# A two-layer graph network on one core: ten of 25 adjacency banks moved beside the products, degrees from one-hots, edge keys by 40 matmuls, x read in fewer pieces

## The chip, the cores and the metric

The kernel runs on one core of a Trainium2 chip. The metric is the device time of one execution in microseconds, the median of several runs. One execution of each kernel is also recorded by the hardware profiler; its page and its trace give the times of single instructions.

## The reference

1250 nodes with 512 features, 20000 edges (`src`, `dst`, sorted by `dst`), two layers. What matters here is the first:

```python
h = jnp.maximum(_layernorm(x, axis=-1), 0.0)          # 1250 x 512
xn = _batchnorm(h, norm1_g, norm1_b)
agg = jax.ops.segment_sum(xn[src], dst, num_segments=N)
deg = jax.ops.segment_sum(jnp.ones((E,)), dst, num_segments=N)
conv_out = relu(agg / jnp.maximum(deg, 1.0)[:, None] @ W_conv + b_conv)
# linear attention (8 heads, random features) over the first 256 nodes: q, k, v from h
x = x + _batchnorm(conv_out + h_attn + h, norm2_g, norm2_b)
# second layer: h = relu(layernorm(x)); z = (1 + eps) h + segment_sum(h[src], dst);
# two dense layers 512 -> 1024 -> 512 with batch norms; x + result
```

The inputs are float32, the indices int32.

## The kernel before

The kernel turns the edge list into a dense matrix `adj` (sources on partitions, 10 blocks of 128 rows; targets on 1250 columns) and does both segment sums as matmuls with it. It is written with a framework that orders each engine's instructions by itself, by their place in the program and a cost model; `order(...)` (`keep_in_program_order`) pins the order where it is used. Buffers come from pools; a tile of a pool with n buffers waits until the tile n before it is no longer used.

**Prologue** (`tile_gnn`, from L1391). The two edge lists are read into `kd` (targets) and `ks` (sources), 125 partitions with overlapping stretches of 400 edges, on the queues of SP and ScalarE. A comparison (`sample`, `less`, L1468 to L1475) and ten matmuls (`cnt`, L1478) find where each of 125 groups of ten targets begins. `pick` (L1495) is a one-hot of these places, and 3 x 20 matmuls `keys` (L1518) gather for each group a slot of 256 edges: the target, the source modulo 128 and the source's block times 1280. `pi` and `ji` (L1490, L1496) split the sources with integer operations on VectorE. VectorE reads the result from PSUM into `kcol` (column key, L1547) and `prow` (row key, L1549). Between these, ScalarE takes the layer norm of the first 256 nodes (`total`, L1506 to L1546), and dummy matmuls (`keep_up`) keep TensorE busy. POOL writes the number lists `iop`, `iok`, `start`, `first` and `lead`.

**Build** (in `sorted_graph`). A batch is a bank of 50 targets, 25 in all. `onehots` (L202) compares the keys with the number lists on VectorE, giving `op` (128x1280, row) and `ok` (128x1000, column); `count` (L213) multiplies them in ten matmuls of 100 columns into a PSUM tile `acc`, and ScalarE copies it into `adj` (L216). The generator `beside()` yields other work in pieces: transposes of the first nodes, the keys of the attention (`features`, L241 to L256) with the layer norm of further nodes (`node`, L95 to L104, transposed at L222), then eight pairs of scores (L263, copied at L329, maximum at L330) with the values (L333), then the queries with the exponentials of the keys (L372). The loop at L393 runs one batch, then a piece, except after every fourth batch; so all 25 batches are written in the program before the last piece ends.

**Products** (L485 to L500). Ten rounds: `query(i)` (scores, L263; exponentials, L457), `product(i)` (block i of xn W_conv, L413, split into `hi` on ScalarE, L109, and `lo` on VectorE, L110), in round 1 the key-value products (L441), then `turn` (L464) and `attend` (L474). `product` has two PSUM buffers of its own (`hw`), in the place that `acc` has left. `add_degrees` (L423) sums the blocks of `adj` on VectorE, and `degrees` (L428 to L430) sums over partitions with a matmul of ones in three pieces, clips and inverts: `rdeg`.

**After that**, the attention's output (L506 to L518), `adj` times `hi` and `lo` (L567), the second layer. `load_x` reads x in blocks of 128 rows, once for `x1` (rows from 256, L166) and once for `xs` (all rows, L528), on SP's queue.

Of the kernel before, what the change touches and what calls it, by code (L numbers as in the profile page):

```python
# [49 lines left out]
LAST = (E - SLOT) // STEP  # L50
JK = 1280
# [17 lines left out]
def sorted_graph(ctx: ExitStack, tc: tile.TileContext, ed, x, n1g, n1b, n2g, n2b, wconv, bconv,  # L69
# [82 lines left out]

    build = ExitStack()
    edge = build.enter_context(tc.tile_pool(name="edge", bufs=1, side="right"))
    ohp = build.enter_context(tc.tile_pool(name="onehot", bufs=2, side="right"))
    accp = build.enter_context(tc.tile_pool(name="acc", bufs=2, space=PSUM))

    def load_x(t, js):
        for j in js:
            nc.sync.dma_start(t[:ROWS[j], j, :], x[j * S:j * S + ROWS[j], :])  # L160
# [5 lines left out]
    load_x(x1, range(NT, NJ))  # L166
# [27 lines left out]
    def onehots(bt, parts=(BG,)):  # L194
        op = ohp.tile([128, BG, S, 2], F16, name="op")
        ok = ohp.tile([128, BG, NJ * TG, 2], F16, name="ok")
        q = 0
        for n in parts:
            qs = slice(q, q + n)
            for t, keys, iota in ((op, prow, ed.iop), (ok, kcol, ed.iok)):  # L200
                shape = [128, n, iota.shape[1], 2]
                i = nc.vector.tensor_tensor(t[:, qs], iota.unsqueeze(1).to_broadcast(shape),  # L202
                                            keys[:, bt, qs].unsqueeze(2).to_broadcast(shape), ALU.is_equal)
                if len(parts) > 1:
                    order(i)
            q += n
        return op, ok

    def count(bt, op, ok):
        acc = accp.tile([S, NJ, TB], F32, name="acc")  # L210
        for q in range(BG):
            for i in range(2):
                nc.tensor.matmul(acc[:, :, q * TG:(q + 1) * TG], op[:, q, :, i],  # L213
                                 ok[:, q, :, i].rearrange("p (j t) -> p j t", t=TG),
                                 start=(q == 0 and i == 0), stop=(q == BG - 1 and i == 1), skip_group_check=True)
        nc.scalar.copy(adj[:, :, bt * TB:(bt + 1) * TB], acc)  # L216
# [172 lines left out]
    rest = beside()  # L389
    nbt = N // TB  # L390
    ahead = onehots(0, (2, 3))
    next(rest)
    for bt in range(nbt):  # L393
        oh, ahead = ahead, onehots(bt + 1, (BG,) if bt else (2, 3)) if bt + 1 < nbt else None
        count(bt, *oh)
        if bt % 4 != 3:
            next(rest, None)
    for _ in rest:
        pass
# [3 lines left out]
    hwp = att.enter_context(tc.tile_pool(name="hw", bufs=2, space=PSUM, reuse_waits="tile"))  # L403
# [3 lines left out]
    def product(j):  # L407

        n = ROWS[j]
        xn = normed(j, nc.scalar) if j not in xns else xns[j]  # L410
        ps = hwp.tile([S, D], F32, name="hw") if j else mm.tile([S, D], F32, name="mm")
        for f in range(KD):
            nc.tensor.matmul(ps[:n], xn[:, f, :n], wct[:, f, :], start=(f == 0), stop=(f == KD - 1))  # L413
        halves(hi[:n, j, :], lo[:n, j, :], ps[:n])


    onesr = ap1.tile([128, 128], F32R, name="onesr")
    nc.gpsimd.memset(onesr.bitcast(F32), 1.0)
    dsum = lop.tile([S, N], F32R, name="dsum")
    rdeg = lop.tile([128, N], F32, name="rdeg")  # L420

    def add_degrees(j):
        nc.vector.tensor_tensor(dsum, (adj[:, 0, :] if j == 1 else dsum).bitcast(F32), adj[:, j, :].bitcast(F32),  # L423
                                ALU.add)

    def degrees(n0, n):
        ps = mm.tile([128, n], F32, name="mm")
        nc.tensor.matmul(ps, onesr, dsum[:, n0:n0 + n], start=True, stop=True)  # L428
        nc.vector.tensor_scalar(rdeg[:, n0:n0 + n], ps, 1.0, None, op0=ALU.max)
        nc.vector.reciprocal(rdeg[:, n0:n0 + n], rdeg[:, n0:n0 + n])  # L430
# [54 lines left out]
    for i in range(len(pairs) + 2):  # L485
        if i < len(pairs):
            query(i)
        product(i)
        if i == 1:
            for q4 in range(2):  # L490
                keyvalue(0, q4)
                keyvalue(1, q4)
        for j in range(2 * i + 1, min(2 * i + 3, NJ)):
            add_degrees(j)
        if 5 <= i < 5 + len(ESPLIT):
            degrees(*ESPLIT[i - 5])
        if 1 <= i <= len(pairs):
            turn(i - 1)
        if i >= 2:
            attend(i - 2)  # L500
# [27 lines left out]
    load_x(xs, range(NJ))  # L528
# [862 lines left out]
def tile_gnn(ctx: ExitStack, tc: tile.TileContext, x, src, dst, *rest):  # L1391
# [5 lines left out]

    ed.iop = pre.tile([128, S, 2], F16, name="iop")
    ed.iok = pre.tile([128, NJ * TG, 2], I16, name="iok")
    ed.prow = pre.tile([128, NGR, 2], F16, name="prow")  # L1400
    ed.kcol = pre.tile([128, NGR, 2], I16, name="kcol")
    ed.x0 = pre.tile([S, NT, D], F32, name="x0")
# [4 lines left out]
    with tc.tile_pool(name="raw", bufs=1) as raw, tc.tile_pool(name="rawp", bufs=1, space=PSUM) as rawp:  # L1407

        kd, ks = (raw.tile([KS, SPAN], I32, name=name) for name in ("kd", "ks"))
        few = E - (KP - 1) * STEP * RB  # L1410

        def edges(queue, t, v, p0, p1, c0, c1):
            at = bass.AP(tensor=v.tensor, offset=v.offset + p0 * STEP * RB + c0, ap=[[STEP * RB, p1 - p0], [1, c1 - c0]])
            order(queue.dma_start(t[p0:p1, c0:c1], at))

        edges(nc.sync, kd, dst, 0, 96, 0, SPAN)
        edges(nc.scalar, kd, dst, 96, KP, 0, few)
        order(nc.vector.memset(kd[96:KP, few:], 0))
        order(nc.vector.memset(ks[96:KP, few:], 0))
        edges(nc.scalar, kd, dst, KP, KS, 0, STEP * RB)  # L1420
        edges(nc.scalar, kd, dst, 96, KP - 1, few, SPAN)
        edges(nc.sync, ks, src, 0, 96, 0, SPAN)
        edges(nc.sync, ks, src, 96, KP, 0, few)
        edges(nc.sync, ks, src, 96, KP - 1, few, SPAN)
# [9 lines left out]
        ones = raw.tile([KS, 128], F16, name="ones")  # L1434
        one = raw.tile([KP, 1], F32, name="one")
        zero = raw.tile([S, 1], F32, name="zero")
        first = raw.tile([KS, NGR + 1], F16, name="first")
        iota(first, [[TG, NGR + 1]])
        for t, v in ((ones, 1.0), (one, 1.0), (zero, 0.0)):
            order(nc.gpsimd.memset(t, v))  # L1440
        start = raw.tile([KP, RB, 2], F16, name="start")
        iota(start, [[1, RB], [0, 2]], step=RB)
        iota(ed.iok, [[JK, NJ], [1, TG], [0, 2]])
        iota(ed.iop, [[1, S], [0, 2]])
        lead = raw.tile([128, NGR], F32, name="lead")
        iota(lead, [[TG, NGR]])
        order(nc.gpsimd.memset(ed.ident, 0.0))
        make_identity(nc, ed.ident, nomemset=True)

        order(nc.vector.memset(ed.epsc, EPS))  # L1450
        order(nc.vector.memset(ed.zeros, 0.0))
# [25 lines left out]
        for b in range(RB):  # L1477
            order(nc.tensor.matmul(cnt, ones, less[:, b, :], start=(b == 0), stop=(b == RB - 1)))  # L1478


        kd16, pk, jk = (raw.tile([KP, SPAN], F16, name=name) for name in ("kd16", "pk", "jk"))
        order(nc.scalar.copy(kd16, kd[:KP]))
        out = raw.tile([KP, few - 1], F16, name="out")
        wrong = raw.tile([KP, 1], F32, name="wrong")
        order(nc.vector.tensor_tensor(out, kd16[:, :few - 1], kd16[:, 1:few], ALU.is_gt))

        pi, ji = (raw.tile([KP, SPAN], I32, name=name) for name in ("pi", "ji"))
        order(nc.vector.tensor_scalar(pi, ks[:KP], S - 1, None, op0=ALU.bitwise_and))  # L1490
        order(nc.scalar.copy(pk, pi))
# [3 lines left out]
        compared(pick, start, begin, ALU.is_equal)  # L1495
        order(nc.vector.tensor_scalar(ji, ks[:KP], 7, None, op0=ALU.logical_shift_right))  # L1496
        order(nc.vector.tensor_reduce(wrong, out, AX.X, ALU.max))
        wps = rawp.tile([1, 1], F32, name="wps")
        keep_up(4)
# [9 lines left out]
        order(nc.scalar.activation(jk, ji, AF.Copy, scale=float(JK)))  # L1509


        keys = rawp.tile([128, 2, 2, NGR], F32, name="keys")
        parts = ((kd16, 0), (pk, 1), (jk, 0))
        for i, (t, kind) in enumerate(parts):
            for h in range(2):
                for b in range(RB):
                    c = STEP * b + 128 * h
                    order(nc.tensor.matmul(keys[:, kind, h, :], t[:, c:c + 128], pick[:, b, :NGR],  # L1518
                                           start=(i == h == b == 0), stop=(t is jk and h == 1 and b == RB - 1),
                                           skip_group_check=True))  # L1520
            if i == 0:
                order(nc.tensor.matmul(wps, wrong, one, start=True, stop=True))
# [11 lines left out]
        total(AF.Square, acc[:, 0:1], 1.0, 1)  # L1534
# [4 lines left out]
        for j in range(NT):  # L1539
# [4 lines left out]
            else:  # L1544
                order(nc.vector.tensor_tensor(nb[:, 0:1], acc[:, 0:1], r, ALU.mult))
            order(nc.scalar.activation(ed.x0[:, j, :], ed.x0[:, j, :], AF.Relu, bias=nb[:, j:j + 1], scale=r))  # L1546
        order(nc.vector.tensor_tensor(ed.kcol, keys[:, 0].rearrange("p h g -> p g h"),  # L1547
                                      lead.unsqueeze(2).to_broadcast([128, NGR, 2]), ALU.subtract))
        order(nc.vector.tensor_copy(ed.prow, keys[:, 1].rearrange("p h g -> p g h")))  # L1549
# [36 lines left out]
```

## Time and profile before

| what | value |
|---|---|
| median of 3 runs | 377.28 us (377.01 to 377.63) |
| profiled execution | 377.67 us, its span 375.9 us |
| TensorE busy | 358.1 us |
| VectorE busy | 245.3 us |
| ScalarE busy | 157.9 us |
| granted TensorE clock, mean | 0.986 |
| prologue, up to the first one-hot | 0 to 11.9 us |
| build, up to the first block of xn W | 11.9 to 67.3 us |
| products | 67.3 to 126.2 us |
| attention's output | 126.2 to 135.3 us |
| sums with `adj`, second layer | 135.3 us to the end |

Each line of a timeline has its start, its length, the engine, the source line, the operation and the tiles. In a table by stage, each engine has its busy time and, in brackets, its number of instructions. In the chain of work that ended last, each line has a start, a length and what ran; "issue" is time in which an engine waited for nothing that the profile shows. PEld is the loading of weights on TensorE, beside its matmuls (PE).

### The profile page before, as it was taken

The page shows a single profiled execution, that of the slowest core. Times are in us where ns is not written, and L with a number is a line of the kernel's source. Part 1 is how long each engine was busy: PE and PEld are TensorE (multiplying, and loading weights), DVE is VectorE, ACT ScalarE, POOL GpSimd, SP SyncE. Part 2 cuts the span into 40 slices and gives each one's busy share as a digit, 9 for nine tenths or more (in the row PEclk, how much of TensorE's full clock was granted, in tenths as well). Part 3 has the DMA queues.
Part 4 walks back from the last instruction along what each step waited for, and adds up shares of the span by engine and source line. Part 5 has one row for each costly group of instructions (what it writes and reads, how often), then busy time and mean ns, then how long its engine had stood idle before and what let it go on. Part 6 is the DMA issues. An engine that isn't in the chain of part 4 may idle for free.

```text
span 375.9 us, 4974 instructions
## 1 busy us (share of the span) xinstructions
PE 358.1 (95%) x1851; PEld 263.5 (70%) x1851; DVE 245.3 (65%) x579; ACT 157.9 (42%) x308; POOL 37.7 (10%) x56
## 2 busy tenths in 40 slices
PE   7799999999999999999999999999999999999971
PEld 4676556485565789998768888777777777777751
DVE  5899999869689227587887232192780888212883
ACT  5599758835664350111157312232652642111230
POOL 4200000000000005000000009610062000000000
PEclk9999999999999999999999999999999999999995
DMA  6853020000000480000000000240000000000045
GB/s 201 265 202 116 2 112 2 1 2 0 1 2 0 165 305 27 3 0 0 2 0 0 2 0 1 57 168 0 2 0 1 1 2 0 1 2 0 13 123 144
DMA packets 13485, 18.06 MB, mean 48 GB/s; under 512 B 1553, under 2 KB 6858, under 8 KB 13454
## 3 DMA queue, kind: packets, MB, share of 16 engines
q1 hardware_dynamic: 10814, 16.38, 12.8%
q10 hardware_dynamic: 2640, 1.29, 1.4%
q8 instruction: 16, 0.26, 0.3%
q14 instruction: 15, 0.12, 0.1%
HBM read 15.11 MB, written 2.56 MB: 47 GB/s over the span
## 4 chain that ended last, share of the span: by engine, by line
PE 82%; DVE 11%; ACT 4%; issue 1%; DMA 1%; DVEq 0%
PE mm L756 29%; PE mm L699 12%; PE mm L567 12%; PE hw L413 9%; PE mm L241 3%; PE mm L513 2%; PE mm L441 2%; PE mm L474 2%; PE sc L263 2%; DVE op L202 1%; PE acc L213 1%; DVE ok L202 1%; DVE xs L886 1%; PE mm L693 1%; PE mm L413 1%
## 5 line engine op out<-in xcount | busy, mean ns | idle before, releaser
L771 ACT ACTIVATE kept<-mm,vT 128x313 f32<-128x313 f32 x36 | 18.5, 521 | 49.6 <-PE mm L756 48.5
L413 PE MATMUL hw<-wconv,xn 128*128 128x512 f32 (+1 forms) x72 | 33.3, 603 | 0.0
L699 PE MATMUL mm<-hi,adj 128*128 128x512 f32 (+2 forms) x100 | 32.1, 398 | 0.5 <-DVE hi L647 0.4
L699 PE MATMUL mm<-lo,adj 128*128 128x512 f32 (+2 forms) x100 | 31.6, 394 | 0.0
L128 ACT ACTIVATE r<-mv,epsc 128x1 f32<-128x1 f32 x16 | 4.7, 292 | 52.7 <-DVE mv L127 52.7
L567 PE MATMUL mm<-adj,hi 128*128 128x416 f32 (+3 forms) x120 | 25.1, 355 | 0.9 <-DVE hT L517 0.9
L756 PE MATMUL mm<-hid,w 128*128 128x313 f32 x96 | 25.8, 427 | 0.0
L567 PE MATMUL mm<-adj,lo 128*128 128x416 f32 (+3 forms) x120 | 25.0, 354 | 0.0
L776 DVE TENSOR_TENSOR hid<-mm,kept 128x313 f32<-128x313 f32 x24 | 10.9, 477 | 20.4 <-ACT kept L771 16.9
L413 PEld LDWEIGHTS hw<-wconv,xn 128*128 128x128 f32 (+1 forms) x72 | 12.7, 187 | 15.4 <-issue 14.7
L567 PEld LDWEIGHTS mm<-adj,hi 128*128 128x128 f32 x120 | 21.8, 189 | 2.4 <-DVE hT L517 1.3
L756 PEld LDWEIGHTS mm<-hid,w 128*128 128x128 f32 x96 | 18.1, 190 | 6.9
L567 PEld LDWEIGHTS mm<-adj,lo 128*128 128x128 f32 x120 | 21.7, 189 | 1.0
L699 PEld LDWEIGHTS mm<-hi,adj 128*128 128x128 f32 (+2 forms) x100 | 18.4, 186 | 5.7 <-DVE hi L647 1.4
L690 DVE SCALAR_TENSOR_TENSOR z<-h,e,mm 128x512 f32<-128x512 f32 (+1 forms) x10 | 7.0, 744 | 23.5 <-PE mm L699 15.7
L699 PEld LDWEIGHTS mm<-lo,adj 128*128 128x128 f32 (+2 forms) x100 | 18.5, 186 | 4.6 <-DVE lo L640 0.2
L202 DVE TENSOR_TENSOR op<-iop,prow 128x1280 f16<-128x1280 f16 (+2 forms) x27 | 20.5, 759 | 0.6 <-PE acc L213 0.4
L213 PEld LDWEIGHTS <-op 128*128 128x128 f16 x250 | 13.5, 97 | 9.6 <-issue 4.5
L776 DVE TENSOR_TENSOR o<-mm,kept 128x313 f32<-128x313 f32 x12 | 5.7, 481 | 21.5 <-ACT kept L771 20.8
L694 ACT COPY zT<-mm 128x512 f32<-128x512 f32 (+1 forms) x10 | 5.3, 582 | 29.2 <-PE mm L693 29.2
L756 PE MATMUL mm<-tz,w 128*128 128x313 f32 x64 | 17.5, 426 | 0.0
L756 PE MATMUL mm<-hid,sw 128*128 128x313 f32 x64 | 17.5, 426 | 0.0
(252 smaller groups left out, 735.4 us busy)
## 6 DMA issues: line engine op xcount, KB each, us to landing
w<-in_L_gnn_W_dram SPq DMA_DIRECT2D x2, 2048.0 KB
x<-in_x_dram SPq DMA_DIRECT2D x9, 256.0 KB
xs<-in_x_dram SPq DMA_DIRECT2D x9, 256.0 KB
wk<-in_L_gnn_Wk_dram SPq DMA_DIRECT2D x1, 1024.0 KB
v<-in_L_gnn_Wv_dram SPq DMA_DIRECT2D x1, 1024.0 KB
wconv<-in_L_gnn_W_conv_dram SPq DMA_DIRECT2D x1, 1024.0 KB
wk<-in_L_gnn_Wq_dram SPq DMA_DIRECT2D x1, 1024.0 KB
o<-in_L_gnn_Wo_dram SPq DMA_DIRECT2D x1, 1024.0 KB
```

The lines of the kernel that those rows point to most:

```text
L202: i = nc.vector.tensor_tensor(t[:, qs], iota.unsqueeze(1).to_broadcast(shape), keys[:, bt, qs].unsqueeze(2).to_broadcast(shape), ALU.is_equal)
L213: nc.tensor.matmul(acc[:, :, q * TG:(q + 1) * TG], op[:, q, :, i], ok[:, q, :, i].rearrange("p (j t) -> p j t", t=TG), start=(q == 0 and i ...
L241: nc.tensor.matmul(ps, wt[:, k, b * 128:(b + 1) * 128], hT[:, k, :TOK], start=(k == 0), stop=(k == KD - 1))
L263: nc.tensor.matmul(ps[:, a, :M], tT[a * 64:a * 64 + 64, b, t * 128:(t + 1) * 128], projT[a * 64:a * 64 + 64, :], start=True, stop=True)
L413: nc.tensor.matmul(ps[:n], xn[:, f, :n], wct[:, f, :], start=(f == 0), stop=(f == KD - 1))
L441: nc.tensor.matmul(ps[:, i, :], kf[:, t, hd, mb * 128:(mb + 1) * 128], va[:, t, hd, :], start=(t == 0), stop=(t == NT - 1))
L474: nc.tensor.matmul(pa[:, i, :], qfTs[n][:, i, mb, :], kv[:, mb, hd, :], start=(mb == 0), stop=(mb == 1))
L567: nc.tensor.matmul(ps, part[:k, j, fs], adj[:k, j, c], start=(part is hi and j == 0), stop=(part is lo and j == NJ - 1))
L699: nc.tensor.matmul(ps[:n], adj[:k, j, t * S:t * S + n], part[:k, j, :], start=(part is hi and j == 0), stop=(part is lo and j == NJ - 1))
L756: order(nc.tensor.matmul(banks[i], left[:, k, m * 128:(m + 1) * 128], right[:, k, i * NH:(i + 1) * NH], start=(p in (1, 2, 5) and k == 0), ...
L771: nc.scalar.activation(t[:, c, :], self.A[c], AF.Identity, bias=self.part(i, 0, c)[1], scale=1.0)
L776: order(nc.vector.tensor_tensor(self.part(i, j, c)[0], self.B[c], t[:, c, :], ALU.add))
```

## The change

Ten of the 25 batches move from the build to the products, one in each round; `op`, `ok` and `acc` outlive the build, and `acc` and the product's `hw` share one tag with two PSUM buffers:

```diff
+    ohp = att.enter_context(tc.tile_pool(name="onehot", bufs=2))
+    accp = att.enter_context(tc.tile_pool(name="acc", bufs=2, space=PSUM))
     build = ExitStack()
...
+    ready = [onehots(0, (2, 3))]
+    def batch(bt):
+        if bt + 1 < nbt:
+            ready.append(onehots(bt + 1, (BG,) if bt else (2, 3)))
+        count(bt, *ready.pop(0))
     next(rest)
-    for bt in range(nbt):
-        oh, ahead = ahead, onehots(bt + 1, (BG,) if bt else (2, 3)) if bt + 1 < nbt else None
-        count(bt, *oh)
-        if bt % 4 != 3:
-            next(rest, None)
-    for _ in rest:
-        pass
+    batches = iter(range(nbt))
+    for piece in itertools.count():
+        if not 6 <= piece < 14 or piece % 2:
+            batch(next(batches))
+        if next(rest, rest) is rest:
+            break
     build.close()
...
-    hwp = att.enter_context(tc.tile_pool(name="hw", bufs=2, space=PSUM, reuse_waits="tile"))
...
-        ps = hwp.tile([S, D], F32, name="hw") if j else mm.tile([S, D], F32, name="mm")
+        ps = accp.tile([S, D], F32, name="hw", tag="acc")
```

The degrees no longer come from `adj` but from one-hots of the targets within their group of ten, six pieces of up to 21 groups in rounds 2 to 7, with `rdeg` in the memory of `wk`:

```diff
-    def add_degrees(j):
-        nc.vector.tensor_tensor(dsum, (adj[:, 0, :] if j == 1 else dsum).bitcast(F32), adj[:, j, :].bitcast(F32), ALU.add)
-    def degrees(n0, n):
-        ps = mm.tile([128, n], F32, name="mm")
-        nc.tensor.matmul(ps, onesr, dsum[:, n0:n0 + n], start=True, stop=True)
-        nc.vector.tensor_scalar(rdeg[:, n0:n0 + n], ps, 1.0, None, op0=ALU.max)
-        nc.vector.reciprocal(rdeg[:, n0:n0 + n], rdeg[:, n0:n0 + n])
+    rdeg = ed.wk.rearrange("p k n -> p (k n)")[:, :N]
+    def degrees(g0, n):
+        shape = [128, n, TG, 2]
+        oh = tmp.tile(shape, F16, name="oh", tag="row")
+        nc.vector.tensor_tensor(oh, ed.iok[:, :TG, :].unsqueeze(1).to_broadcast(shape),
+                                ed.dist[:, g0:g0 + n].unsqueeze(2).to_broadcast(shape), ALU.is_equal)
+        ps = mm.tile([128, n * TG], F32, name="mm")
+        for i in range(2):
+            nc.tensor.matmul(ps, ed.ones, oh[:, :, :, i].rearrange("p g t -> p (g t)"), start=(i == 0), stop=(i == 1))
+        c = slice(g0 * TG, (g0 + n) * TG)
+        nc.vector.tensor_scalar(rdeg[:, c], ps, 1.0, None, op0=ALU.max)
+        nc.vector.reciprocal(rdeg[:, c], rdeg[:, c])
...
-        for j in range(2 * i + 1, min(2 * i + 3, NJ)):
-            add_degrees(j)
-        if 5 <= i < 5 + len(ESPLIT):
-            degrees(*ESPLIT[i - 5])
+        if 2 <= i < 8:
+            degrees(21 * (i - 2), min(21, NGR - 21 * (i - 2)))
+        for bt in itertools.islice(batches, 1):
+            batch(bt)
```

In the prologue the source is gathered once, as source/128, and split after the matmuls by rounding; a first matmul with one row adds the offsets that `lead` held. ScalarE makes the two 16-bit lists in two pieces each, one `keep_up` matmul of four goes, the prologue's PSUM tiles move to the other end of PSUM, and ScalarE keeps the targets' distances (`dist`):

```diff
-    parts = ((kd16, 0), (pk, 1), (jk, 0))
-    ... (20 matmuls for each of the three)
+        halved(kd16, kd, 1.0)
...
+        halved(ks16, ks, 1.0 / S)
+        order(nc.tensor.matmul(keys, ed.ones[0:1, :], lead, start=True, stop=False, skip_group_check=True))
+        keep_up(3)
...
+        for kind, t in enumerate((ks16, kd16)):
+            ... (20 matmuls for each of the two)
...
-        order(nc.vector.tensor_tensor(ed.kcol, keys[:, 0].rearrange("p h g -> p g h"),
-                                      lead.unsqueeze(2).to_broadcast([128, NGR, 2]), ALU.subtract))
-        order(nc.vector.tensor_copy(ed.prow, keys[:, 1].rearrange("p h g -> p g h")))
+        order(nc.vector.tensor_scalar(js, part, 1.5 * 2 ** 23, -1.5 * 2 ** 23, op0=ALU.add, op1=ALU.add))
+        order(nc.vector.scalar_tensor_tensor(ed.prow, js, -1.0, part, op0=ALU.mult, op1=ALU.add))
+        order(nc.vector.scalar_tensor_tensor(ed.kcol, js, float(JK), dist, op0=ALU.mult, op1=ALU.add))
+        order(nc.scalar.copy(ed.dist, dist))
```

The integer operations `pi` and `ji` and their copies go. The lists with every number twice (`iop`, `iok`, `start`) are now written once by POOL and doubled by VectorE copies. The edge lists are read with 112 partitions on SP and 13 on ScalarE's queue (96 and 29 before).

x is read in fewer pieces:

```diff
-    load_x(x1, range(NT, NJ))
+    load_x(x1, (NT, NT + 1), (NT + 1, NT + 3), (NT + 3, NJ - 1))
...
-    load_x(xs, range(NJ))
+    load_x(xs, (0, NJ - 1))
```

with one read for each group and one for the last, shorter block.

## The prediction

> **What bounds the kernel now.** I read the page's busy times first, then the busy times by stage, then the chain of work that ended last, and last the timelines of TensorE, VectorE and ScalarE over the first 136 us, the only part that the change touches (after that it alters only how x is read back and where `rdeg` lies).
>
> ```profile
> span 375.9 us, 4974 instructions
> PE 358.1 (95%) x1851; PEld 263.5 (70%) x1851; DVE 245.3 (65%) x579; ACT 157.9 (42%) x308; POOL 37.7 (10%) x56
> ```
>
> TensorE looks full, but its matmul spans overlap (an `acc` matmul shows 205 ns and the next starts 46 to 50 ns later). So I work with start-to-start times. By stage:
>
> ```profile
> 11.91:15.29 3.38, 2.46 (x26) 2.17 (x27) 3.38 (x9) 1.93 (x4) 0.01 (x1) 1.00 0.95 327
> 15.29:31.86 16.57, 15.95 (x121) 11.54 (x121) 15.89 (x43) 13.93 (x33) 0.55 (x5) 1.00 0.64 224
> 31.86:51.34 19.48, 19.20 (x158) 10.83 (x157) 19.33 (x38) 14.44 (x28) 0.23 (x2) 1.00 0.07 24
> 51.34:67.34 16.00, 14.92 (x120) 10.03 (x120) 15.95 (x40) 11.94 (x28) 0.00 (x0) 1.00 0.17 65
> 67.34:126.17 58.83, 58.83 (x283) 35.98 (x284) 44.30 (x85) 32.06 (x76) 0.00 (x0) 1.00 0.00 1
> ```
>
> Columns after the stretch's length: PE, PEld, DVE, ACT, POOL, clock, DMA. From 11.91 to 67.34 (the build: adjacency, first norm, keys, values, queries) VectorE is busy nearly all the time; in the product stage (67.34 to 126.17) TensorE alone is. The clock is full throughout. The chain says the same. In the prologue it is the key matmuls, then two VectorE reads of their bank, then the one-hots:
>
> ```profile
> 7.30 1.16 PE keys L1518 x20
> ...
> 8.57 2.39 PE keys L1518 x40
> 11.05 0.43 DVE kcol L1547
> 11.91 0.42 DVE op L202
> ```
>
> In the build it runs over VectorE for 14 us, then over ScalarE:
>
> ```profile
> 34.97 0.72 DVE op L202
> 35.76 0.59 DVE ok L202
> 36.35 0.60 DVE kmx L330
> ...
> 60.90 0.51 ACT kf L372
> 61.41 0.46 ACT adj L216
> 61.87 0.28 ACT qT L245
> ```
>
> In the product stage it is TensorE without a gap; one round is
>
> ```profile
> 100.55 3.63 PE hw L413 x8
> 104.36 0.44 PE mm L464 x4
> 104.80 0.84 PE mm L474 x8
> 105.64 0.63 PE sc L263 x4
> ```
>
> 5.54 us, plus 0.19 in the three rounds with a degree matmul.
>
> **How much room the build has.** TensorE's work from 11.91 to 67.34, by start-to-start times: L241 64 x 0.2165 = 13.9; L244/L249 16 x 0.265 = 4.2; scores 9 x 0.63 = 5.7; L333 16 x 0.46 = 7.4; transposes of nodes 1.0 + 8 x 0.5 = 5.0; small ones 1.3; 240 `acc` matmuls x 0.048 = 11.5. Sum 48.9 of 55.4: 6.5 us in which TensorE waits (about 1.4 before 15.29, 1.0 to 31.9, 1.6 to 51.3, 2.5 to 67.3). That slack is all the move can win; the `acc` matmuls themselves only change place.
>
> **The change, part by part.**
>
> *Ten banks moved.* A bank costs TensorE 10 x 0.048 = 0.48, VectorE 0.73 + 0.59 = 1.32 (op, ok), ScalarE 0.47 (adj copy). One already ran beside the products (69.25), so nine leave the build: -4.3 us of TensorE there, +4.3 in the product stage. VectorE's load in the build falls by 11.9. What is late next: in the pairs (31.9 to 51.3) the scores have one buffer, and a pair is scores 0.70, copy 0.58, maximum 0.68, about 2.1 us with handovers, against 1.6 to 2.1 of TensorE work; in the queries it is ScalarE, which has its 16 exponentials (0.40 each), a table load of 1.28 and nearly as many bank copies per step as before. So I take 4.3 of the 6.5 us of slack as staying (bounds 1.5 and 6.0), and 2.2 as won.
>
> *Does the product stage hide the moved work?* TensorE does not: it pays. VectorE: 44.3 busy, minus nine sums L423 at 1.37 (12.3), plus nine one-hot pairs at 1.32 (11.9), plus the degree edits below (about 2.8) gives 47 of some 63 us. ScalarE 32.1 + 9 x 0.47 = 36. Neither binds on average. Blocks of xn W and banks now share two PSUM buffers, so in steady rounds block i+1 waits until `lo` of block i is read. In round 95 to 101 block i ended at 98.6 and `lo` at 99.97, 1.4 us later; the next block comes 0.44 + 0.84 + 0.63 = 1.9 us after the end today, and 2.4 with a bank between. A margin of 1.0 us: VectorE is a queue in order, and a one-hot (0.73) in front of `lo` fits, a one-hot and a reciprocal of half length (1.37) do not. Bounds 0 and 0.5 us per round; I take 0.4 in all, nearest to rounds 85 to 95, where VectorE was 92 to 100% busy with the sums and the chain stayed on TensorE.
>
> *Row and rule on small matmuls.* Ten `acc` matmuls between fp32 work took 0.46 to 0.57 us in the chain. The Trainium skill, "TensorE: Matmul & The Clock Gate", section "Back-to-back issue gap", speaks against moving them onto a full TensorE: weight load and matmul pairs sustain about 81 ns each at 128 columns, because the load counts too; by it a bank would be an estimated 0.8 us and the moved nine 7.3 rather than 4.3. The rows show 46 to 57 ns each, loads included, so the sum goes by them.
>
> *Degrees.* Removed: nine sums (VectorE, above), three matmuls at 0.18 on TensorE (-0.5), a POOL memset. Added: 12 matmuls of 210 columns, scaled from the 100-column `acc` (0.048) about 0.09 each, +1.1; six comparisons 128x420 (row: ok 128x400, 0.36) 2.1; the maximum and reciprocal in six pieces for three, 0.6 more of overhead. TensorE +0.5; VectorE's part lies in its free 16 us.
>
> *Keys.* 20 of 60 matmuls go: 20 x 0.060 = -1.2. In: one matmul on one row for the offsets (500 columns, 0.2 to 0.36) against one of four fillers at 0.36, and the check's matmul (0.12) moves ahead: keys start about 0.15 later than 7.30, end about 9.85 instead of 10.96. Then three VectorE reads of 250 elements (js, prow, kcol; nearest rows 0.41 and 0.42, 0.37 start to start) where two stood: +0.37. One-hots start near 11.15 instead of 11.91: -0.75. Cover: the pair lists now come from VectorE copies (0.2 to 0.3 each) after shorter POOL iotas, in VectorE's 2.0 us of idle time before `sample` at 3.46; if the iotas cost like `iop`'s 1.51 rather than `lead`'s 0.24, `sample` slips by up to 0.5. Bounds -1.1 and -0.2. Without the collision of the key banks with `mm`, the first transposes (11.94, just after `prow` ends) can start about 1 us earlier; I count this within the 2.2.
>
> *The copy of distances on ScalarE.* It reads the bank that VectorE reads three times. In the rows the two never read one bank at once: the copy of scores ends at 38.58, the maximum starts at 38.89. The Trainium skill, "PSUM — Partial Sum Buffer", section "PSUM bank collisions raise a hardware error", says two engines must not touch one bank and quadrant together, so the copy stands behind the last read. By the row that is 0.4 us at about 11.1 to 11.5, needed only by the degrees after 70 us and by the bank's next owner; on the path it would add 0.4, I count nothing.
>
> *Loads.* Eight reads of x become four, ten become two, the same bytes. SP issues the first in 1.7 instead of 3.81 us; `wv` and what follows start 2 us earlier. Rows 5 to 8 land together, by about 17.5 at the 327 GB/s of the stretch, and are first read at 21.3. The second set is wanted at 154.65 and issued at 125.41. No path: 0; if one landed late, the norm of a node (0.7) would slip.
>
> **Sum**, against the profiled execution, 377.67 us (span 375.9 and 1.8 around it), 0.39 above the median 377.28: keys -0.75, slack -2.2, degrees +0.5, stalls of the products +0.4: -2.05, so 375.6 there and 375.2 as a median.
>
> **Rivals.**
> (1) Larger gain: VectorE was the only brake, and the scheduler fills the rest with work of later stages, as it already did with the query scores at 54.42. Slack kept 1.5, no stalls: -0.75 - 5.0 + 0.5 = -5.25, 372.0. Against it: the ScalarE chain at 59 to 67.
> (2) A wash: score loop and ScalarE hold the build, slack kept 6.0: -0.75 - 0.5 + 0.5 + 0.4 = -0.35, 376.9. For it: the chain leaves VectorE at 48.2 already.
> (3) Slower: the shared PSUM buffers. If `lo` stands behind a one-hot and a reciprocal, it ends 1.4 + 0.73 + 1.37 = 3.5 after its block, 1.1 after the next could start, in rounds with degrees; at a mean of 0.5 over nine rounds +4.5 in place of 0.4, +2.05 in all, 379.3. It decides from 0.27 us a round on.
> That the scheduler pulls moved banks back into the build is possible too: then both stages change less, between (2) and the forecast.
>
> **How the numbers follow.** Forecast 0.52, (1) 0.16, (2) 0.14, (3) 0.18. Likeliest case alone, slack kept 3 to 5.5, keys -0.2 to -1.1: 373.4 to 376.7. Range 371.8 to 378.8: it takes in (1), (2) and the milder half of (3). A measurement tells 0.2% (0.75 us) from no change. Faster: 0.48 of the forecast, all of (1), a quarter of (2): 0.68. Same: 0.13. Slower: 0.19.
>
> **What would show it.** Right: one-hots start at 11.0 to 11.4; the first block of xn W starts about 7 us earlier than 67.34; rounds are about 6.0 us, 6.2 with degrees, with no idle before `hw`; the chain stays on TensorE from there. Wrong: `hw` waiting for `lo` (rival 3); a build that shrinks by under 5 us (rival 2) or over 9 (rival 1); `sample` later than 3.5; a wait for x before L95.

## The result

| | kernel before | changed kernel |
|---|---|---|
| median of 12 runs each, us | 377.61 (377.01 to 378.09) | 376.34 (375.83 to 378.15) |
| profiled execution, us (span) | 377.67 (375.9) | 377.66 (375.9) |
| first one-hot starts at | 11.91 | 12.14 |
| from there to the first block of xn W | 55.4 | 51.0 |
| on to the first transposes of the attention's output | 58.7 | 64.0 |
| on to the first sum with `adj` | 9.28 | 8.06 |

The change makes the kernel faster by a ratio of 0.9975 (95% interval 0.996 to 0.9989): 0.25%, about 1 us, where 375.2 us and thus over 2 us were forecast. The profiled executions of both are equal, and the one of the changed kernel is among the longer of its 12 (eight lie at 375.83 to 376.55, four at 377.04 to 378.15). Why they scatter is a finding of its own, below. By stage, the profiled executions differ by +0.23, -4.36, +5.23 and -1.22 us, and by +0.1 in all that follows.

### The profile page after: what moved, and what is told of

The parts are those of the page before. It is cut to its first block, busy times and chain, and to the rows that moved or that the text cites. A ratio compares the mean times of both kernels' runs of the same rounds, so it can differ in the third digit from the quotient of the medians.

```text
span 375.9 us, 4922 instructions
## 1 busy us (share of the span) xinstructions
PE 357.0 (95%) x1840; PEld 263.3 (70%) x1840; DVE 235.6 (63%) x585; ACT 157.4 (42%) x310; POOL 35.4 (9%) x55
## 4 chain that ended last, share of the span: by engine, by line
PE 83%; DVE 11%; ACT 2%; issue 1%; DMA 1%; DVEq 0%
PE mm L764 29%; PE mm L707 12%; PE mm L575 12%; PE hw L422 10%; PE mm L245 3%; PE mm L449 2%; PE mm L521 2%; PE mm L482 2%; PE sc L267 2%; PE acc L217 2%; DVE op L206 1%; DVE xs L894 1%; PE mm L226 1%; PE mm L701 1%; DVE kmx L334 1%; PE mm L472 1%
## 5 line engine op out<-in xcount | busy, mean ns | idle before, releaser
L422 PE MATMUL hw<-wconv,xn 128*128 128x512 f32 (+1 forms) x80 | 37.1, 605 | 0.3 <-ACT adj L220 0.3
L422 PEld LDWEIGHTS hw<-wconv,xn 128*128 128x128 f32 (+1 forms) x80 | 14.1, 188 | 16.4 <-issue 14.8
L217 PE MATMUL acc<-ok,op 128*128 128x100 f16 x250 | 16.2, 208 | 3.4 <-DVE ok L206 2.7
```

## The profile after

The head of the page. TensorE lost 1.1 us of busy time and VectorE 9.7, and the span did not move:

```profile
span 375.9 us, 4922 instructions
PE 357.0 (95%) x1840; PEld 263.3 (70%) x1840; DVE 235.6 (63%) x585; ACT 157.4 (42%) x310; POOL 35.4 (9%) x55
```

Busy times by stage of the changed kernel (start:end, length, then PE, PEld, DVE, ACT, POOL, granted clock, DMA share, GB/s). The third line is the stage of the score pairs, the fourth that of the queries:

```profile
12.14:15.53 3.39, 1.56 (x18) 1.26 (x19) 3.39 (x9) 2.30 (x5) 0.00 (x0) 1.00 1.00 324
15.53:31.64 16.11, 15.48 (x111) 11.07 (x111) 15.51 (x44) 13.37 (x31) 0.66 (x6) 1.00 0.64 215
31.64:52.86 21.22, 19.24 (x135) 10.80 (x135) 20.65 (x51) 13.83 (x30) 0.11 (x1) 1.00 0.19 68
52.86:63.15 10.29, 10.03 (x60) 6.26 (x60) 4.68 (x12) 7.26 (x17) 0.00 (x0) 1.00 0.01 2
63.15:127.11 63.96, 63.96 (x383) 40.66 (x383) 46.02 (x103) 37.12 (x86) 0.00 (x0) 1.00 0.01 1
```

VectorE lost a fifth of its work in the build (44.2 of 51.0 us busy, before 54.6 of 55.4). But it is not relieved where it is needed: in the pairs it is still busy for 20.65 of 21.22 us, and then it has 4.68 us of work in 10.29. The one-hots in the pairs did shrink (`op` and `ok` together from 14.8 to 9.6 us), but the framework's order drew other work into the room: the statistics `gst` went from 2.9 to 4.6 us, and the normalised blocks `xn` (2.1 us) and two comparisons of the new degrees (`oh`, 0.75 us) came in. The chain of work that ended last shows what this does (start, length, engine, tile and line):

```profile
43.24 0.77 DVE op L206
44.01 0.60 DVE kmx L334
44.61 0.59 DVE ok L206
...
45.91 0.86 DVE xn L289 x3
46.77 0.60 DVE kmx L334
47.36 0.73 DVE op L206
48.09 0.59 DVE ok L206
48.69 0.60 DVE xn L289 x3
49.28 0.09 issue
49.37 0.69 DVE kmx L334
50.06 0.73 DVE op L206
50.79 0.59 DVE ok L206
51.38 0.74 DVE op L206
52.12 0.61 DVE kmx L334
52.73 0.14 issue
52.86 0.70 PE sc L267 x4
```

Between two key maxima `kmx` stand the one-hots of a bank and the normalised blocks `xn`, 2.6 to 2.9 us from one maximum to the next. The scores have one PSUM buffer, and it is free when the maximum has been read. So TensorE gets on at VectorE's pace. In its timeline the wait stands in brackets:

```profile
50.11 0.70 PE L267 MATMUL sc<-projT,kT 64*128 64x256 f32 x4 [0.45 <-DVE kmx L334]
...
52.86 0.70 PE L267 MATMUL sc<-projT,qT 64*128 64x256 f32 x4 [0.80 <-DVE kmx L334]
```

A few us later VectorE is out of work, since TensorE has not yet used the one-hots that it made (two buffers); its timeline:

```profile
61.84 0.82 DVE L206 TENSOR_TENSOR op<-iop,prow 128x1280 f16<-128x1280 f16 x1 [5.23 <-PE acc L217]
```

In the products the chain is TensorE alone. A round with a degree piece is 6.20 us, the bank (`acc`) 0.46 and the degrees (L435) 0.19 of it, and nothing stands before `hw`:

```profile
99.24 3.63 PE hw L422 x8
102.87 0.19 PE mm L435 x2
103.06 0.46 PE acc L217 x10
103.52 0.45 PE mm L472 x4
103.97 0.84 PE mm L482 x8
104.81 0.63 PE sc L267 x4
```

## The experiments

Each edit is to the changed kernel unless said otherwise. The letters in an expectation are its own; they do not name the same theory from one to the next. The stage of each run is told as the time from its first one-hot to the first transposes of the attention's output ("build and products"): 114.10 us in the kernel before, 114.97 in the changed one.

**The changed kernel again.** No edit.

> The changed kernel once more, for a second profile. Clock theory: its 12 times fall in two groups (375.8 to 376.6 and 377.0 to 378.2) because the key matmuls run at half clock in some executions (in the profile of after 20 of them took 102 ns each, in the profile of before 60 ns); so a profile with one-hots starting before 11.4 us has a span near 374.2, one with a start after 12 near 375.9. Rival: the spread comes from the moved banks or from memory; then spans differ with the same start of the one-hots.

Measured: 377.34 us (375.84 to 378.23, 12 runs), ratio 0.9989 (0.9975 to 1.0004), so less of a gain than in the first runs. This profile has its first one-hot at 10.31, not 12.14. TensorE's timelines of the prologue show why, first in the first profile of the changed kernel, then in this one:

```profile
4.46 1.21 PE L1498 MATMUL cnt<-less,ones 125*128 125x126 f16 x10 [0.52 <-DVE less L1488]
...
7.50 2.21 PE L1528 MATMUL keys<-pick,ks 124*128 124x125 f16 x20
9.55 1.29 PE L1528 MATMUL keys<-pick,kd 124*128 124x125 f16 x20
```

```profile
4.60 0.73 PE L1498 MATMUL cnt<-less,ones 125*128 125x126 f16 x10 [0.67 <-DVE less L1488]
...
6.59 1.30 PE L1528 MATMUL keys<-pick,ks 124*128 124x125 f16 x20
7.72 1.30 PE L1528 MATMUL keys<-pick,kd 124*128 124x125 f16 x20
...
13.70 3.38 PE L245 MATMUL mm<-hT,wk 128*128 128x256 f32 x8
```

The same matmuls start every 102 ns (2.05 us for 20) in the one and every 57 ns in the other: little more than half the speed. The second execution gives 1.4 of its 1.8 us back later, where eight L245 take 3.38 us instead of 1.97 after the first one-hots. The granted clock in the stage table reads 1.00 in both prologues, but shows the later case:

```profile
13.70:17.08 3.38, 3.38 (x11) 2.55 (x12) 2.27 (x6) 0.29 (x1) 0.00 (x0) 0.56 0.98 337
```

So single executions differ by where TensorE runs at about half speed, and such a phase costs 1.4 to 1.8 us here, which is more than the change is worth. The span of 374.2 us that was expected with an early start was missed (375.3), because of this later phase.

**The new prologue alone, on the kernel before.** All of the diff in `tile_gnn`; the 25 banks, the degrees from `adj` and the loads as before.

```diff
 (kernel before)
-        parts = ((kd16, 0), (pk, 1), (jk, 0))
+        for kind, t in enumerate((ks16, kd16)):
 ... and the rest of the prologue's diff
```

> Before, with only the new prologue (40 key matmuls, split after the gather, doubled lists from VectorE, distances copied by ScalarE). Clock theory: 0.3 to 0.8 us faster than before in the median, and its times scatter over 1 to 2 us like those of the changed kernel. Rival (the scatter belongs to the moved banks): a steady 0.75 us faster, within 0.6 us of each other as before.

Measured: 376.31 us (375.95 to 379.13, 12 runs), ratio 0.998 (0.9963 to 0.9998); eight runs lie at 375.95 to 376.55, four at 377.94 to 379.13. The profiled one, 377.94, is of the latter: one-hots at 12.33, `keys<-pick,ks` again at half speed (2.31 us). Build and products took 114.13, as before. The times scatter as the clock theory said, without the moved banks. Within that scatter the prologue alone gives all that the whole change gives.

**All 25 banks back in the build.**

```diff
-    batches = iter(range(nbt))
-    for piece in itertools.count():
-        if not 6 <= piece < 14 or piece % 2:
-            batch(next(batches))
-        if next(rest, rest) is rest:
-            break
+    batches = iter(range(0))
+    for bt in range(nbt):
+        batch(bt)
+        if bt % 4 != 3:
+            next(rest, None)
+    for _ in rest:
+        pass
```

> The changed kernel with all 25 banks in the build, in the order of before. Theory A (the move wins nothing in the build, because the scores' single buffer and VectorE's queue hold it; nine banks cost TensorE 4.2 us in the products and free 4.4 in the build): within 0.7 us of the changed kernel. Theory B (the forecast: the move wins 2.2 us of slack): 1.5 to 2.5 us slower than the changed kernel. Theory C (the move costs): over 0.7 us faster than it.

Measured: 377.91 us (376.18 to 379.28, 12 runs), ratio 0.9996 (0.998 to 1.0012). By stage, build and products took 115.09, against 114.97 with ten banks moved: the move by itself is worth 0.1 us. The times of this run and of the changed kernel (377.34 in the run above) scatter too much over the prologue's two speeds to say more.

**One dummy matmul more ahead of the keys, two more at the start.**

```diff
-        keep_up(6)
+        keep_up(8)
...
-        keep_up(3)
+        keep_up(4)
```

> The changed kernel with eight dummy matmuls instead of six ahead of the counting matmuls and four instead of three ahead of the keys, so that TensorE has no gap of 0.5 us at 3.9 us. Clock theory: the keys run at 60 ns each in the profile, one-hots start at 11.0 to 11.5 us, times in one group near 375.8 to 376.3 (0.5 to 1 us below the changed kernel's mean). Rival (the clock does not depend on this, or the extra dummies delay the keys by as much): no difference or up to 0.4 us slower.

Measured: 376.41 us (376.15 to 378.52, 6 runs), ratio 0.9968 (0.9955 to 0.9981). In its profile the counting matmuls are still slow (1.21) but `pick,ks` is not (1.30); one-hots at 11.39. Then eight L245 took 3.28 us at 14.78, and this execution was the longest, 378.52. Half a remedy.

**Dummy matmuls also between the first one-hots.**

```diff
+    keep_up(4, sc.tile([128, 2, 512], F32, name="sc")[:, 0, :])   # ahead of the build's loop
...
-        keep_up(6)
+        keep_up(8)
...
-        keep_up(3)
+        keep_up(2)
...
+        keep_up(4)                                                 # after the keys
```

> The changed kernel with dummy matmuls where TensorE waits around the keys: eight instead of six ahead of the counting matmuls, two instead of three ahead of the keys, four after the keys, four after the first transposes. Clock theory (the executions near 377 to 378 us are those in which TensorE falls back to half speed, at the keys in the profile of after, at the first L245 matmuls in that of again, 422 ns each for 216): one group of times near 375.8, at most one in four above 377; L245 at 216 ns. Rival (the slow group has another cause): two groups as before, half of the times above 377.

Measured: 376.55 us (376.13 to 377.93, 10 runs), ratio 0.9968 (0.9956 to 0.9979); nine of ten below 376.8. One-hots at 10.44. The one long execution is the profiled one, and it has its slow phase elsewhere, after three waits for VectorE:

```profile
48.68 0.70 PE L267 MATMUL sc<-projT,kT 64*128 64x256 f32 x4 [0.40 <-DVE kmx L334]
50.01 0.63 PE L217 MATMUL acc<-ok,op 128*128 128x100 f16 x10 [0.62 <-DVE ok L206]
51.43 0.78 PE L267 MATMUL sc<-projT,qT 64*128 64x256 f32 x4 [0.79 <-DVE kmx L334]
...
52.31 3.40 PE L245 MATMUL mm<-hT,wk 128*128 128x256 f32 x8
```

So most of the scatter goes when the short waits are filled. That every long execution has a half-speed phase is seen only in those that were profiled, one of each run; for the others it is inferred.

**The same dummies on the new prologue alone.**

```diff
 (kernel before, with the new prologue)
+ the four keep_up edits of the run above
```

> Before, with only the new prologue and the same dummy matmuls as fill_all. The difference to fill_all is what the moved banks, the new degrees and the fewer loads are worth at full clock. Theory A (the move wins nothing in the build; degrees cost 0.6; the output stage, which starts its sums 1.2 us earlier, pays for it): within 0.6 us of fill_all. Theory B (the forecast, move worth 2.2 - 0.5 - 0.4): 1.3 us or more slower than fill_all.

Measured: 375.94 us (375.26 to 376.39, 6 runs), ratio 0.9956 (0.994 to 0.9972). That is 0.6 us less than with the whole change (376.55), where theory B wanted at least 1.3 us more. With the same dummies in both, moved banks, degrees and loads together bring nothing. One thing in it I had not asked for: its output stage is 8.06 us, as in the changed kernel, with one more tile `sc` and none of the moved work.

**Two tiny writes to two more tiles of `mm`, on the kernel before.**

```diff
 (kernel before, ahead of the attention's output)
+    for _ in range(2):
+        nc.vector.memset(mm.tile([128, 512], F32, name="mm")[:, :1], 0.0)
```

> Before, with two small writes to two more tiles of the pool mm ahead of the attention's output, so that its four buffers are taken in the turn that the changed kernel has (six degree pieces for three, block 0 no longer there: two more modulo four). Theory: the first sum with adj no longer waits for the last hT (0.87 us idle before 135.29), the stretch from the first L506 to the first L567 falls from 9.28 to about 8.1, the time by 1.0 to 1.2 us. Rival (the stage is shorter for another reason): no change.

Measured: 376.34 us (375.93 to 377.6, 7 runs), ratio 0.9963 (0.995 to 0.9976). The end of the output stage on TensorE, in the kernel before, in the changed kernel, and here:

```profile
135.29 2.19 PE L567 MATMUL mm<-adj,hi 128*128 128x418 f32 x10 [0.87 <-DVE hT L517]
```

```profile
135.17 2.26 PE L575 MATMUL mm<-adj,hi 128*128 128x418 f32 x10
```

```profile
135.37 2.25 PE L569 MATMUL mm<-adj,hi 128*128 128x418 f32 x10
```

The first sum with `adj` takes its buffer in memory that older PSUM pools have left. Before, it waited until VectorE had read the last `hT` from a buffer of `mm`. Six degree pieces in place of three, and block 0 no longer in `mm`, shift the turn of `mm`'s four buffers by two, and the wait of 0.87 us is gone; two empty tiles do the same. That the turn is what did it in the changed kernel too is inferred from this run; in `prologue_fill` the wait is gone without a tile more in `mm`, and what did it there stays open. The stage falls from 9.28 to 8.06 us. 0.87 of that is the wait. The other 0.35 is overlap: up to the end of the last product the stages are alike (8.41 us in the kernel before, 8.42 here), and without the wait the first sum starts 0.36 us before that end. The changed kernel got this 1.2 us by accident.

**The key maximum from ScalarE's copy**, with the dummies of `fill_all` in place. ScalarE copies the scores to `kf` in SBUF anyway; read from there, the PSUM buffer is free after the copy and no longer waits for VectorE's queue.

```diff
-            nc.vector.tensor_reduce(kmx[:, t, o:o + 2], ps, AX.X, ALU.max)
+            nc.vector.tensor_reduce(kmx[:, t, o:o + 2], kf[:, t, o:o + 2, :], AX.X, ALU.max)
```

> fill_all, with the maximum of the scores read from ScalarE's copy in SBUF instead of from PSUM, so that the next scores wait for that copy alone and not for VectorE's queue. Theory A1 (the single score buffer, freed behind VectorE's queue, holds the pairs): the stretch from the first values (L337) to the first block of xn W shrinks by 1.5 to 2.5 us, and the time falls by as much, to about 373.8. Rival A2 (VectorE's load itself, or ScalarE in the queries, holds it): below 0.5 us.

Measured: 372.93 us (372.69 to 373.15, 4 runs), ratio 0.9872 (0.9853 to 0.9892), the best of all and 3.6 us below `fill_all`. From the first value matmul (L337) to the first block of xn W it took 29.2 us, in `fill_all` 33.25, of which about 1.4 was the slow phase, so a little over the 1.5 to 2.5 us of theory A1. Build and products: 111.75. So the score buffer did hold the changed kernel's build. Two things remained open: whether it had held the kernel before as well, and what the move is worth without it.

**The same with all 25 banks back in the build.**

> The run kmx_fill (the changed kernel, more dummy matmuls, key maximum from ScalarE's copy in SBUF, 372.93 us) with 25 banks left in the build as in the kernel before. It asks what the move of the banks is worth once VectorE's queue no longer frees the score buffer. Theory A (the score loop held the build's length, so the move won nothing while it stood): without that loop TensorE's own work sets the build, nine banks that leave it shorten it by their 4.3 us and cost 4.1 to 4.3 us later, so first one-hot to L514 stays within 0.6 us of kmx_fill's 111.75, time 372.5 to 373.6. Theory B (the move wins slack as the prediction had it, and the loop hid that): with the loop gone VectorE's 11.9 us of one-hots come back into the build as the bound, first one-hot to L514 at least 1.5 us longer, time 374.4 or more.

Measured: 376.66 us (376.37 to 377.5, 10 runs), ratio 0.998 (0.9971 to 0.999), build and products 115.41. Theory A fell, B held: 3.7 us are lost again. The build by stage (10.33 to 67.86):

```profile
10.33:29.43 19.10, 17.85 (x145) 12.83 (x142) 19.00 (x52) 15.83 (x37) 0.66 (x6) 1.00 0.70 243
29.43:48.50 19.07, 18.98 (x149) 11.33 (x148) 18.38 (x35) 13.79 (x28) 0.12 (x1) 1.00 0.09 33
48.50:67.86 19.36, 17.73 (x150) 12.32 (x149) 19.11 (x49) 14.88 (x34) 0.00 (x0) 1.00 0.16 55
```

VectorE is busy for 56.5 of 57.5 us: with 25 banks its whole load is the bound, whoever frees the score buffer.

**The key maximum from the copy, on the kernel before**, nothing else.

> The kernel before with one edit: the key maximum is taken from ScalarE's copy of the scores in SBUF instead of from the PSUM bank, so that the score buffer comes free after the copy. Theory A: the same loop set the length of the build before the change, so it shortens here too, by 2 to 4 us: first block of xn W at 63.3 to 65.3 instead of 67.3, time 373.7 to 375.7. Theory B: in the kernel before VectorE's whole load (one-hots of 25 banks) was the bound of the build, and the loop only after the move: first block at 66.8 or later, time 376.8 to 377.6.

Measured: 378.05 us (377.29 to 378.25, 10 runs), ratio 1.0011 (1.0002 to 1.0021), build and products 114.49, first block at 67.77. Theory A fell here too: no gain, rather 0.4 us lost, which I can't explain. The scores come closer together (2.43 us from one to the next, before 2.73), but VectorE is busy for 54.5 of the build's 55.75 us, with all the one-hots to do.

**The key maximum from the copy, on the changed kernel**, nothing else: the fourth corner.

> The changed kernel with the key maximum from ScalarE's copy in SBUF, and nothing else: the fourth corner beside the kernel before, the changed kernel and kmx_before. Theory C (two limits of nearly the same length, VectorE's load with 25 banks and the score buffer that VectorE's queue frees; the move takes the first, the edit the second, and only both together shorten the build): first one-hot to L514 111.2 to 112.5 as in kmx_fill (111.75) against 114.97 in the changed kernel, 372.4 to 374.0 us by the clock of the prologue. Theory D (the dummy matmuls of kmx_fill made its gain, by the clock): 114 or more, time 375.5 to 376.5.

Measured: 374.89 us (373.37 to 375.04, 4 runs), ratio 0.9926 (0.99 to 0.9953). Build and products took 112.19, within the 111.2 to 112.5 of theory C. The time lies above its 372.4 to 374.0: in the profiled execution `pick,ks` ran at half speed again and the one-hots began at 12.02. The build by stage:

```profile
12.02:31.40 19.38, 16.90 (x129) 12.25 (x129) 18.77 (x52) 15.50 (x37) 0.66 (x6) 1.00 0.66 233
31.40:45.00 13.60, 13.60 (x82) 6.95 (x81) 13.39 (x35) 10.29 (x21) 0.11 (x1) 1.00 0.09 33
45.00:60.67 15.67, 15.67 (x116) 10.44 (x116) 11.82 (x28) 11.64 (x27) 0.00 (x0) 1.00 0.18 68
```

From 31.40 to the first block TensorE has no gap. VectorE is as full in the pairs as it was (13.39 of 13.60), but no longer in TensorE's way. Scores start 2.11 us apart, in the changed kernel 2.83. The framework orders the other instructions anew with the edit, so the gain is that of the edit with its new order. Build and products of all corners, us:

| | maximum from PSUM | maximum from the copy |
|---|---|---|
| kernel before (25 banks in the build) | 114.10 | 114.49 |
| changed kernel with 25 banks in the build | 115.09 | (with dummies) 115.41 |
| changed kernel, 15 banks in the build | 114.97 | 112.19 (with dummies 111.75) |

From the 115.09 of the second row, the move alone gives 0.1 us, the edit alone (with dummies) loses 0.3, and both together give 2.9. From the kernel before, both give 1.9: the changed kernel with 25 banks in the build is itself 1.0 us longer there, 0.6 of it from the degrees.

## Why the prediction was half right

**The step that failed: "2.2 as won" of the build's slack.** The build did shrink, by 4.4 us, but that is only the nine banks' own 4.1 to 4.3, paid again in the products. Of the slack nothing was won: 0.1 us (115.09 to 114.97). The prediction's own sign for this, "a build that shrinks by under 5 us (rival 2)", came true. The mistake is in one line of the working: "a pair is scores 0.70, copy 0.58, maximum 0.68, about 2.1 us with handovers". That is what a pair takes if VectorE reads each score bank at once. It does not: the maximum stands in VectorE's queue behind one-hots and statistics, and the scores follow each other at 2.83 us. The trace of before showed 2.73 (scores at 34.28 to 50.63, six intervals), so the 2.1 could have been checked against it. 2.11 is what the pairs take once the buffer no longer waits for VectorE (32.60 to 45.26 in the corner with both edits). First and seventh scores, kernel before, then that corner:

```profile
34.28 0.70 PE L263 MATMUL sc<-projT,kT 64*128 64x256 f32 x4
...
50.63 0.70 PE L263 MATMUL sc<-projT,kT 64*128 64x256 f32 x4
```

```profile
32.60 0.70 PE L267 MATMUL sc<-projT,kT 64*128 64x256 f32 x4
...
45.26 0.70 PE L267 MATMUL sc<-projT,kT 64*128 64x256 f32 x4
```

With that edit the move wins what was forecast: the build goes from 55.36 to 48.65 us, 6.7, against the predicted 4.3 + 2.2.

So the diagnosis was right, the bound was VectorE, and taking work from it was not enough. A second limit of almost the same length, the buffer that VectorE's queue frees, stood behind the first. Rival (2) named this loop and was given 0.14. Its other half, ScalarE, did not show: in the corner with both edits TensorE has no gap, with ScalarE's load unchanged. The moved work left VectorE idle after the pairs (5.23 us) instead of relieving it within them.

**Keys, "-0.75".** In the profiled execution +0.23, because TensorE ran at half speed from the counting matmuls to the 20 `pick,ks`; where it is at full speed from the counting on, the one-hots begin at 10.3 to 10.5, which is -1.4 to -1.6. The bounds -1.1 to -0.2 missed both. The prediction took the keys' 60 ns from one execution, and its "clock is full throughout" from a table that begins at 11.91 us; for the first 10 us the granted clock would not have told it, the starts of the matmuls do. In the kernel before, the counting matmuls already started 102 to 106 ns apart, and only the keys ran at full speed. Two runs of the new prologue are like that, `warm` and `kmx_fill`: their one-hots begin at 11.39 and 10.89, -0.5 and -1.0, inside the bounds, though with other numbers of dummies. The rest of that step stands: three reads of the bank from 10.88 to 12.1, `sample` at 3.38, under the 3.5 named as a limit.

**Degrees, "+0.5".** Six pieces at 0.19 against three: +0.6. Right.

**Stalls of the products, "+0.4", and rival (3).** The rounds are the sum of their parts, 5.54 + 0.46 + 0.19 = 6.20 (rounded parts). One wait of 0.25 us for ScalarE's copy of `adj` stands before the first `hw`. The shared buffers cost nothing else; rival (3) is refuted.

**Small matmuls.** Ten in 0.46 us, on a TensorE with no gap. The 81 ns that the Trainium skill, "TensorE: Matmul & The Clock Gate", section "Back-to-back issue gap", states for each at 128 columns would, by an estimate, have made the nine banks 7.3 us instead of 4.1. The rows decide, and the choice for them was right.

**ScalarE's copy of the distances** began at 12.17, just after VectorE's last read of that bank, and delayed nothing that the chain shows. The first transposes start at 10.69 instead of 11.94, as foreseen, but won nothing: the chain goes from the one-hots over `acc` (15.21) to the first L245 (15.53). **Loads**: no wait for x; 0, as said.

**Not foreseen: -1.22 us in the output stage**, most likely from the turn of `mm`'s buffers. The prediction's sum has no term past 126 us. Of the gain of about 1 us it is the larger part: build and products cost 0.87, the output stage gives 1.22, and the keys give or cost something by the clock. So that the kernel became faster, as forecast, is in good part luck. That the eight shorter runs owe their 1.5 us to a prologue at full speed (+0.87 - 1.22 - 1.5 = -1.85, about what separates their 376.0 from 377.6) is worked out from the other runs' profiles; none of those eight was profiled.

## What to carry to other kernels

Taking load from a full engine shortens nothing while the next engine's buffers are freed by instructions that stand in that engine's queue: look at the interval between two uses of the buffer in the trace, not at the sum of the steps in it, and read from the copy that another engine makes anyway. When an edit brings nothing, try it together with the one that opens the next limit before calling it useless; here each alone gave 0.1 us or less and both together 2.9. And a change in the number of tiles drawn from a rotating pool can shift a wait in a stage that nobody touched.

## What was not expected of the hardware

TensorE's half-speed phases decide 1.4 to 1.8 us of an execution of this kernel. In the first 10 us they show only in the distance of starts (102 ns instead of 57 for 125 columns), while the granted clock reads 1.00; that these are the same thing as the later ones is inferred from the like slowing. Later ones show in that column (0.56 where eight L245 take 3.38 us instead of 1.97). The Trainium skill, "TensorE: Matmul & The Clock Gate", section "What's actually happening", puts such phases down to a clock gate that goes by TensorE's activity in a free-running window of about 3.4 us, so that the moment of the change varies from run to run; the scatter here fits that. It also gives a whole idle window as the condition, while here waits of 0.40, 0.62 and 0.79 us within 3.2 us stood before the phase at 52.3. They do not always suffice: the first profile of the changed kernel has waits of 0.45, 0.62 and 0.80 us at the same place and runs its next eight L245, at 53.60, in 1.89 us.

The maximum of 512 fp32 columns takes VectorE 0.67 us from SBUF and 0.68 from PSUM, so reading the copy costs no more than reading the bank.
